# The last sequence through every expert with gates, the one before it in a group of three, and the retention's values multiplied once

## The chip, the cores and the metric

The kernel runs on one core of a Trainium2 chip. Its time is the device time of one execution in microseconds (us). Three runs of the kernel before took 1190.32, 1191.34 and 1193.39 us; the median is 1191.34. The profile is of one further execution, traced by the hardware profiler. PE is the engine that multiplies matrices, DVE the vector engine, ACT the scalar engine with its function tables, POOL the general engine that also issues the indirect transfers, and SP the queue that issues most other transfers. PSUM is the memory that PE writes here, and from which DVE and ACT read.

## The reference, cut to what matters

Sixteen sequences of 256 rows and 128 features go through two layers. Each layer is a mixer and an expert part, with a shift, a scale and a gate per sequence around both (adaLN).

```python
# layer 0: retention with 8 heads of 16, then experts that choose their rows
S = g * S + k_t[..., :, None] * v_t[..., None, :]
y_t = jnp.einsum('bhde,bhd->bhe', S, q_t)
...
top_p, top_idx = jax.lax.top_k(probs_et, cap)            # each of 8 experts takes 64 of 256 rows
...
# layer 1: a selective scan (256 inner features, 16 states), then rows that choose two experts
h = dA * h + dt_t[..., None] * b_t[:, None, :] * u_t[..., None]
y = jnp.einsum('bdn,bn->bd', h, c_t)
...
h = rms_weight * (x * jax.lax.rsqrt(var + EPS))
logits = jnp.einsum('bsh,eh->bse', h, gate_w)
top_w, top_i = jax.lax.top_k(scores, TOP_K)              # 2 of 8
top_w = top_w / jnp.sum(top_w, axis=-1, keepdims=True)
cw = jnp.einsum('tke,tk->te', oh, top_w.reshape(-1, TOP_K))   # weight of every expert for every row
a = jnp.einsum('th,eih->eti', hf, w1)
g = jnp.einsum('th,eih->eti', hf, w3)
eo = jnp.einsum('eti,ehi->eth', jax.nn.silu(a) * g, w2)
out = jnp.einsum('eth,te->th', eo, cw)
```

In this last part the weight of an expert that a row did not choose is zero, so a kernel may compute the chosen two experts only, or all eight and multiply by the weight.

## The kernel before, in words

**How the order of the work is set.** The program is written as chains (`pl.chain`), each with a number from the table `U`. A chain is a list of instructions; `need` names an event that must have happened, `done` announces one, and `take` and `give` hand buffers around as tokens. `Plan.issue` (line 320) goes through all chains with a time for every instruction from the table `USUAL`, always issues what can start first, and among what can start within 0.15 us on that engine takes the chain with the lowest number. The outcome is one fixed order per engine. Where PE would be idle beyond an allowance, it puts matmuls of zeros (line 384) in; these stop after the last sum of the scans (`h.pad = False`, line 1514).

**Layer 0.** Sequences go in four groups of four. `scores(b)` (line 773) makes queries and keys with features on the partitions, and the values with rows on the partitions. A head has 16 features, and the kernel multiplies in blocks of 32 partitions, so two heads share a block: the keys are masked once for the even and once for the odd heads (`ke`, `ko`), and the values are needed twice as well, with the other head's columns at zero. Before, the value weights are laid out twice (`wveo`, made by POOL in line 717, 256 columns), so that the product `pv` comes out as [even heads, odd heads] with zeros; ACT copies all 512 elements to `v`. The state between the two chunks of 128 rows is `kd` times the even half plus `kd` times the odd half, two matmuls (lines 826 and 827). `outputs0` (line 862) takes blocks of 32 columns of `v`. The expert part follows (`choose`, `gather`, `hidden`, `outputs`, `scatter`).

**Layer 1, scan.** `front(b)` makes the scan's inputs, `scans` (line 1413) runs 256 steps of 128 by 512, sixteen to a sequence, in order of the sequences: ACT makes `dA`, POOL `dB`, DVE scans in place and multiplies by C, and PE sums (`ya`). `back(k)` (line 1525) handles the pair of sequences 2k and 2k+1: projection, norm and residual. Its statistics are DVE's; the reciprocal root (`inv_std`, line 543: two instructions and three Newton steps of four) and the additions to `X` are POOL's.

**Layer 1, experts.** `GROUPS` (line 32) collects the pairs: 0 to 5 by two, and 6 and 7 alone. `prepare(k)` (line 1565) makes the pair's normed rows, the squares' mean with a second reciprocal root, the rows `hs` to be sent and the logits. `route(g)` (line 1619) picks two experts per row and gives every row a place in a list sorted by expert, padded to tiles of 128 rows: with c chunks of 128 rows there are 2c + 7 tiles. `send(g)` (line 1698) scatters the rows to DRAM by 2c indirect transfers. `expert(g, j)` (line 1723) loads one tile, transposes it, multiplies by `w1` and `w3` of the tile's expert (PE reads its number into a register), forms the gated product (`sl`, two buffers; ACT's tanh, two DVE instructions), transposes it in four pieces (`pm`, copied to `mT`, two buffers), multiplies by `w2`, and stores 128 rows. Odd tiles of the last group use the PSUM banks that the scans have left. `combine(k)` (line 1803) gathers each row's two results by indirect transfers, weighs and adds them and stores the output. The groups have 8, 8, 8, 4 and 4 chunks, so 23, 23, 23, 15 and 15 tiles, 99 in all.

The three lines that set the groups and tiles are these:

```python
GROUPS = ((0, 1), (2, 3), (4, 5), (6,), (7,))
CGS = [len(ks) * T // P for ks in GROUPS]
NJS = [2 * c + E - 1 for c in CGS]
```

## Time and profile before

| what | value |
|---|---|
| median of 3 runs | 1191.34 us |
| profiled execution, its own time | 1200.99 us |
| its span, first to last instruction | 1199.0 us |
| PE busy | 1059.6 us (88%), of it matmuls of zeros in the scans 153.5 us |
| DVE busy | 888.1 us (74%) |
| ACT busy | 764.3 us (64%) |
| POOL busy | 784.2 us (65%) |
| first scan starts | 230.7 us |
| last scan and its product end | 1041.6 us |
| 64 scatters, 64 gathers (indirect, POOL) | 64.9 us, 62.1 us |
| last tile's product stored from | 1177.1 us |

Busy times of engines overlap. A busy PE is not PE at its peak, because matmuls are pipelined and their ends are modelled; the distance between two starts says more. The clock is the share of full speed that PE was granted. Idle time of an engine that nothing waits for costs nothing. In rows of instructions the columns are start, duration, engine, line, operation, what is written from what, shape and count; many rows carry line 237, the helper that records every operation, so they are told apart by the names of their tiles.

### The profile page before, as it was taken

The numbers are of one execution on the slowest core, as the hardware profiler recorded it, in microseconds if no ns is written. First come the engines' busy times: TensorE is split into PE (matmuls) and PEld (weight loads), VectorE is DVE, ScalarE is ACT, GpSimd is POOL, SyncE is SP. The second block draws the span as 40 slices with busy tenths as digits, with TensorE's granted clock in tenths as the row PEclk, the third lists the DMA queues.
The fourth block names the chain that finished last, engine by engine and source line by source line (L and its number), as shares of the span: only waits on it lengthen the run. The fifth ranks groups of instructions, "written<-read, shape, count | busy, mean of one in ns | idle before, by whom it ended". The sixth has DMA issues, their size and how long they took to land.

```text
span 1199.0 us, 23439 instructions
## 1 busy us (share of the span) xinstructions
PE 1059.6 (88%) x7589; PEld 757.8 (63%) x7589; DVE 888.1 (74%) x1835; ACT 764.3 (64%) x1717; POOL 784.2 (65%) x1307
## 2 busy tenths in 40 slices
PE   9999999989898898799797898899988999988882
PEld 7767687767475665566565566667655766565661
DVE  5688804888989679977877897889878899835331
ACT  4555546677686787647755776678765786564451
POOL 4532303668685789569786888786886888664355
PEclk9999999999998999899899999899999999999996
DMA  6108232784585946656549652446334555221222
GB/s 198 16 28 223 86 108 80 192 207 141 144 220 145 280 124 152 167 145 176 147 124 226 169 135 74 112 133 162 103 91 121 155 141 134 80 63 51 73 73 59
DMA packets 122355, 157.61 MB, mean 131 GB/s; under 512 B 18756, under 2 KB 92300, under 8 KB 121868
## 3 DMA queue, kind: packets, MB, share of 16 engines
q1 hardware_dynamic: 117004, 140.90, 44.3%
q0 software_dynamic: 4096, 8.40, 2.7%
q10 hardware_dynamic: 1136, 6.82, 1.8%
q8 instruction: 64, 1.05, 0.4%
q14 instruction: 55, 0.45, 0.1%
HBM read 128.11 MB, written 27.96 MB: 130 GB/s over the span
## 4 chain that ended last, share of the span: by engine, by line
PE 44%; DVE 23%; POOL 10%; issue 8%; ACT 8%; DMA 6%; another core or an unknown queue 0%; SPq 0%; POOLq 0%; DVEq 0%; ACTq 0%
DVE dB L237 10%; PE py L1787 5%; PE pa L1757 5%; PE ya L237 4%; PE pg L1757 4%; PE ya L384 3%; PE pxs L237 3%; DMA rep<-dd 3%; DMA pr<-spd 2%; PE pm L237 2%; PE ph L237 2%; POOL dB L237 2%; DVE sl L237 2%; PE pye L237 2%; PE py L237 2%
## 5 line engine op out<-in xcount | busy, mean ns | idle before, releaser
L237 POOL TENSOR_TENSOR dB<-rep,bt 128x512 f32<-128x512 f32 x256 | 327.9, 1303 | 98.2 <-PE ya L237 71.4
L237 DVE TENSOR_TENSOR_SCAN dB<-dA,dB 128x512 f32<-128x512 f32 x256 | 310.2, 1216 | 52.9 <-ACT dA L237 25.9
L237 ACT ACTIVATE dA<-rep,A 128x255 f32<-128x255 f32 x512 | 222.2, 470 | 91.6 <-DVE dB L237 86.4
L384 PE MATMUL ya<-nought 128*128 128x256 bf16 x1122 | 153.5, 284 | 20.9 <-DVE dB L237 20.9
L237 DVE TENSOR_TENSOR dB<-dB,ct 128x512 f32<-128x512 f32 x256 | 168.6, 670 | 1.3 <-PE ct L237 1.1
L384 PEld LDWEIGHTS <-nought 128*128 128x128 bf16 x1270 | 129.1, 103 | 54.9 <-DVE dB L237 23.1
L1787 PEld LDWEIGHTS py<-w,mT 112*128 112x128 f32 x792 | 98.9, 192 | 49.2 <-ACT mT L237 26.5
L1787 PE MATMUL py<-w,mT 112*128 x792 | 108.6, 281 | 21.5 <-ACT mT L237 12.8
L237 DVE SCALAR_TENSOR_TENSOR sl<-sl,pa 128x448 f32<-128x448 f32 x99 | 60.9, 615 | 65.4 <-ACT sl L237 48.1
L1757 PE MATMUL pa<-w,xT 128*128 x198 | 97.8, 576 | 7.7 <-issue 2.5
L237 POOL DMA_INDIRECT got<-ydr,pos x64 | 62.1, 970 | 54.1 <-issue 19.4
L1757 PE MATMUL pg<-w,xT 128*128 x198 | 91.6, 544 | 0.0
L237 ACT ACT_TABLE_LOAD x66 | 84.7, 1283 | 10.8 <-DVE dB L237 4.4
L1705 POOL DMA_INDIRECT disp<-hs,pos x64 | 64.9, 1014 | 37.9 <-DVE pos L237 15.5
L237 PE MATMUL ya<-dB,c 128*32 128x512 f32 x512 | 78.8, 635 | 9.9 <-DVE dB L237 7.8
L237 ACT COPY mT<-pm 112x512 f32<-112x512 f32 x99 | 57.7, 584 | 35.0 <-PE pm L237 24.4
L237 DVE TENSOR_TENSOR sl<-sl,pg 128x448 f32<-128x448 f32 x99 | 61.5, 621 | 9.5 <-PE px L237 0.2
L237 ACT ACTIVATE sl<-pa 128x448 f32<-128x448 f32 x99 | 53.2, 542 | 23.2 <-PE pa L1757 18.7
L237 ACT ACTIVATE yt<-py 128x128 f32<-128x128 f32 x99 | 27.2, 276 | 62.8 <-PE py L1787 44.6
L237 PE MATMUL ph<-xin,fw 128*128 128x256 f32 x256 | 65.4, 391 | 1.0 <-ACT xin L237 0.8
L237 PE MATMUL pye<-fw,hg 128*64 128x128 f32 x1024 | 63.1, 276 | 0.5 <-ACT hg L237 0.5
L237 PE MATMUL pm<-c,sl 128*112 128x128 f32 x396 | 61.7, 276 | 1.4 <-ACT yt L237 0.7
(322 smaller groups left out, 2151.2 us busy)
## 6 DMA issues: line engine op xcount, KB each, us to landing
rep<-dd SPq DMA_DIRECT2D x128, 512.0 KB
fw<-in_fw SPq DMA_DIRECT2D x64, 256.0 KB
gt<-spd SPq DMA_DIRECT2D x64, 128.0 KB
pr<-spd SPq DMA_DIRECT2D x64, 128.0 KB
dd<-dx SPq DMA_DIRECT2D x16, 512.0 KB
xt<-disp SPq DMA_DIRECT2D x99, 64.0 KB
ydr<-yt SPq DMA_DIRECT2D x99, 64.0 KB
w<-in_w ACTq DMA_DIRECT2D x3, 1792.0 KB
```

What stands on the lines that cost most here:

```text
L237: i = getattr(real, name)(*args, **kw)
L384: self.nc.tensor.matmul(pad[:, 0:256], self.nought, self.spare, start=False, stop=False, skip_group_check=True)
L1705: i = nc.gpsimd.indirect_dma_start(out=disp[g], out_offset=bass.IndirectOffsetOnAxis(ap=pos[g][:, c, r, :], axis=0), in_=hss[GROUPS[g][c / ...
L1757: nc.tensor.matmul(o, xT, w[:, bass.ds(which[0], 1), :].rearrange("p o i -> p (o i)"), start=True, stop=True)
L1787: nc.tensor.matmul(py, mT[:, ic, :], w2[:, bass.ds(which[0], 1), ic, :].rearrange("p o d -> p (o d)"), start=(ic == 0), stop=(ic == NFC - 1),)
```

## The change

Three things change, and with them the table `U`.

- The pairs become a list: seven pairs, then sequence 14 alone and sequence 15 alone (`PAIRS`; nine entries). The fourth group takes pair 6 and sequence 14, so 6 chunks and 19 tiles. Sequence 15 is in no group. `back`, `prepare` and `combine` work on one or two sequences.
- Sequence 15 goes through `every_expert`: no routing, no scatter, no gather. Both of its chunks go through all eight experts, 16 products, each weighed by the gate, which is zero for experts that a row did not choose, and all summed in one PSUM bank. The rows' reciprocal root is not applied to the rows ahead of `w1` and `w3` but put into the tanh's scale (`half`) and the gate. For this sequence the reciprocal roots and additions of `back` and `prepare` run on DVE in place of POOL. The 69 tiles of the first three groups stay; with 19 and 16 there are 104.
- The values are multiplied once: the product has 128 columns, and ACT puts even and odd heads into a buffer [even, zeros, odd] whose zeros are written once. Blocks [even, zeros] and [zeros, odd] are read as overlapping slices. The state is one matmul.
- All numbers of `U` are other ones. The small buffers of statistics over two chunks have one copy in place of two (`few`). Odd tiles of the last group take the transposition's bank from `ps_y` in place of `ps_c`, which now holds the dense sum.

The diff, cut to its core:

```diff
+PAIRS = tuple((2 * k, 2 * k + 1) for k in range(7)) + ((14,), (15,))
+NB = len(PAIRS)
-GROUPS = ((0, 1), (2, 3), (4, 5), (6,), (7,))
+GROUPS = ((0, 1), (2, 3), (4, 5), (6, 7))
...
-         rep=50.85, exp=32.88, dB=104.34, ct=434.95, sum=89.24, scan=422.0, hC=369.42, yg=-40.53,
+         rep=242.95, exp=221.94, dB=152.25, ct=623.44, sum=-12.0, scan=527.94, hC=397.52, yg=31.12,
...
-CGS = [len(ks) * T // P for ks in GROUPS]
+CGS = [sum(len(PAIRS[k]) for k in ks) * NCH for ks in GROUPS]
...
-    wveo = fixed1(at, [P, 2, D], "wveo")
+    vz = [fixed1(at, [P, NCH, 4, 3, DH], f"v{i}") for i in range(2)]
...
+            for v in vz:
+                G.memset(v[:, :, :, 1, :], 0.0)
...
                 T_.matmul(
-                    pv[:, ch, :], hT[:, ch * P : (ch + 1) * P], wveo.rearrange("p q d -> p (q d)"),
-                    start=True, stop=True, us=0.43,
+                    pv[:, ch].rearrange("p j q e -> p (j q e)"), hT[:, ch * P : (ch + 1) * P], wv,
+                    start=True, stop=True, us=0.25,
                 )
-            v = vs[b] = at.tile([P, NCH, 2 * D], F32, tag="v", name=f"v{b}")
-            S.copy(v, pv)
+            v = vs[b] = vz[b % 2]
+            S.copy(
+                v[:, :, :, 0:3:2, :].rearrange("p c j q e -> p (c j) q e"), pv.rearrange("p c j q e -> p (c j) q e"), us=0.42
+            )
...
-            T_.matmul(pk[:, 1, :], kd, v[:, 0, 0:D], start=True, stop=False, us=0.25)
-            T_.matmul(pk[:, 1, :], kd, v[:, 0, D : 2 * D], start=False, stop=True, us=0.25)
+            T_.matmul(pk[:, 1, :], kd, v[:, 0, :, 0:3:2, :], start=True, stop=True, us=0.25)
...
-                            py[r, ch, :], vs[b][:, ch, par * D + 32 * j : par * D + 32 * j + 32], prs[b, j][:, ch, par, :],
+                            py[r, ch, :], vs[b][:, ch, j, par : par + 2, :].rearrange("p q e -> p (q e)"), prs[b, j][:, ch, par, :],
...
     def back(k):
+        W, kind = (V, "late") if k == NB - 1 else (G, None)
...
     def prepare(k):
+        dense = k == NB - 1
+        W, kind = (V, "late") if dense else (G, None)
...
+        if dense:
+            xTd = fa.tile([P, n * L], F32, tag="xTd", name="xTd", bufs=1)
+            S.activation(xTd, hT, AF.Copy, scale=rms)
+            done("xTd")
...
+    def every_expert(k, got):
+        xTd, lg, rr = got
+        b = PAIRS[k][0]
+        pl.chain(U['gated'])
+        need(("lg", k))
+        m8, i8 = fs.tile([P, NCH, 8], F32, tag="dm8", name="dm8"), fs.tile([P, NCH, 8], U32, tag="di8", name="di8")
+        for c in range(NCH):
+            V.max(m8[:, c, :], lg[:, c, :])
+            V.max_index(i8[:, c, :], m8[:, c, :], lg[:, c, :], us=0.3)
+        half, d2, ws, w0 = (fs.tile([P, NCH], F32, tag=t, name=t) for t in ("dhalf", "dd2", "dws", "dw0"))
+        V.tensor_scalar(half, rr, 0.5, None, ALU.mult)
+        done("half")
...
+        for r, (o, w) in enumerate(((gate, w0), (part, d2))):
+            V.tensor_tensor(o, iF[:, :, r].unsqueeze(2).to_broadcast([P, NCH, E]), io, ALU.is_equal)
+            V.tensor_tensor(o, o, w.unsqueeze(2).to_broadcast([P, NCH, E]), ALU.mult)
+        V.tensor_tensor(gate, gate, part, ALU.add)
+        for f in (rr, half):
+            V.tensor_tensor(gate, gate, f.unsqueeze(2).to_broadcast([P, NCH, E]), ALU.mult)
+        done("gate")
+        acc = ps_c.tile([P, NCH, D], F32, tag="c", name="accd")
+        for e in range(E):
+            for c in range(NCH):
+                n = NCH * e + c
+                pl.chain(U['dense'] + n / 100)
+                need("xTd", "half", "weights", ("yg", B - 1))
...
+                if n:
+                    need(("begun_", n - 1))
+                x = xTd[:, c * P : (c + 1) * P]
+                T_.matmul(pa, x, w1[:, e, :], start=True, stop=True)
+                done(("begun_", n))
+                T_.matmul(pg, x, w3[:, e, :], start=True, stop=True)
+                sl = fa.tile([P, FI], F32, tag="sl", name=f"sl_{n}")
+                S.activation(sl, pa, AF.Tanh, scale=half[:, c : c + 1])
+                V.scalar_tensor_tensor(sl, sl, 1.0, pa, ALU.add, ALU.mult)
+                give(ta)
+                need("gate")
+                V.scalar_tensor_tensor(sl, sl, gate[:, c, e : e + 1], pg, ALU.mult, ALU.mult)
...
+                for ic in range(NFC):
+                    T_.transpose(pm[:, ic, :], sl[:, ic * FC : (ic + 1) * FC], ident, us=0.16)
...
+                S.copy(mT, pm)
...
+                for ic in range(NFC):
+                    T_.matmul(
+                        acc[:, c, :], mT[:, ic, :], w2[:, e, ic, :], start=(n == 0 and ic == 0),
+                        stop=(e == E - 1 and ic == NFC - 1), skip_group_check=True,
+                    )
+                done(("dense", n))
+        pl.chain(U['dense'] + 1)
+        need(("dense", NCH * E - 1), ("x2", k))
...
+        V.tensor_tensor(res, acc, both(tab[:, 0, :]), ALU.mult, kind="fres")
+        V.tensor_tensor(res, res, X[b], ALU.add, kind="late")
+        Q.dma_start(rows_of((b,)), res)
...
-        for k in range(NHS, NB):
+        for k in range(NHS, NB - 1):
             prepare(k)
+        every_expert(NB - 1, prepare(NB - 1))
```

The numbers of `U` that the prediction speaks of order the tail: `tile` is (164.88, 54.77, 166.68, 110.24, -86.25) before and (328.09, 371.73, 101.71, -70.25) after, `dense` is -39.78 and `gated` -57.2.

## The prediction

> **What bounds the kernel now.** I read the sums by stage first, with stretches cut at the first scan (230.7 us), at the scan steps of sequences 13, 14 and 15, at the last scan's end (1040.4), at the first expert tile of the last group (1122) and at the last tile's end (1177). Columns: stretch, its length, busy us of PE, weight loads, DVE, ACT, POOL, then granted clock, DMA share, GB/s.
>
> ```profile
> core 0: us, PE busy (x) PEld busy (x) DVE busy (x) ACT busy (x) POOL busy (x), PEclk, DMA share, GB/s
> 0.00:230.70 230.70, 221.93 (x2173) 171.14 (x2174) 142.12 (x487) 124.33 (x266) 80.33 (x282) 1.00 0.40 112
> 230.70:867.70 637.00, 559.80 (x3871) 400.20 (x3870) 534.86 (x909) 452.21 (x976) 487.41 (x722) 0.96 0.60 158
> 867.70:937.90 70.20, 61.52 (x331) 39.91 (x330) 55.98 (x121) 43.62 (x108) 52.22 (x60) 0.98 0.42 112
> 937.90:989.20 51.30, 48.72 (x290) 33.10 (x289) 45.07 (x73) 40.39 (x100) 44.78 (x68) 1.00 0.56 145
> 989.20:1040.40 51.20, 47.68 (x273) 31.03 (x272) 48.78 (x101) 32.57 (x85) 40.17 (x52) 1.00 0.41 109
> 1040.40:1122.00 81.60, 71.21 (x395) 48.33 (x393) 37.25 (x106) 40.81 (x107) 40.48 (x84) 1.00 0.22 59
> 1122.00:1177.00 55.00, 48.77 (x267) 34.10 (x265) 22.24 (x41) 28.52 (x74) 25.39 (x29) 1.00 0.29 78
> 1177.00:1199.00 22.00, 0.00 (x0) 0.00 (x0) 1.76 (x5) 1.83 (x6) 13.48 (x16) 0.54 0.21 57
> ```
>
> Three regimes. Up to the first scan PE is full (222 of 231 us, DVE 62%). The scans, 810 us for 16 sequences, 50.6 each, are shared by PE, DVE and POOL; in the last step DVE has 48.8 of 51.2 us. After the last scan come 159 us in which DVE is under half busy and PE works on expert tiles, and 22 us at the very end in which PE does nothing at all.
>
> PE's instructions in the retention's steady loop show why its first stage is full: nothing stands between them but 0.18 us.
>
> ```profile
> 29.65 0.61 PE L237 MATMUL pk<-v,kd 128*128 128x128 f32 x4
> 30.10 0.60 PE L237 MATMUL pqk<-hTa,pk 128*128 128x256 f32 x2
> 30.53 1.03 PE L237 MATMUL pv<-wveo,hTa 128*128 128x256 f32 x4
> 31.39 0.38 PE L237 MATMUL pta<-c,xna 128*128 128x128 f32 x2
> 31.95 0.64 PE L237 MATMUL py<-pr,v 128*32 128x128 f32 x16 [0.18 <-ACT ko L237]
> ```
>
> From start to start the value projection takes 30.53 to 31.39, 0.86 us, and the state product 29.65 to 30.10, 0.45 us.
>
> The tile rows give the tail's load: 35 tiles after 1040.4, of them 16 after 1122.
>
> ```profile
> L237 ACT COPY mT<-pm x35: 562/586/590, 1045.2 to 1174.9; 112x512 f32<-112x512 f32 x35
> L237 ACT COPY mT<-pm x16: 573/586/590, 1126.4 to 1174.9; 112x512 f32<-112x512 f32 x16
> ```
>
> The chain of the tail, cut to what ended late, shows one tile's PE pieces and what the last group waits for.
>
> ```profile
> 1087.16 0.81 PE pl L237 x8
> ...
> 1121.80 0.30 PE px L237
> ...
> 1126.03 0.75 PE pg L1757 x2
> 1126.78 0.44 PE pm L237 x4
> 1127.32 0.76 PE pa L1757 x2
> 1128.08 0.75 PE pg L1757 x2
> 1128.83 0.89 PE py L1787 x8
> ```
>
> The gate's matmuls of sequences 14 and 15 (pl) end at 1088; the first tile's transpose starts 34 us later. Between lie the routing (8 us of small DVE instructions), eight scatters and the way through DRAM. Then 16 tiles run at 48.5/15 = 3.23 us each, while their PE pieces sum to 0.76 + 0.75 + 0.44 + 0.89 + 0.11 = 2.95. Behind the last one stand the gathers:
>
> ```profile
> 1177.07 1.53 DMA ydr<-yt
> ...
> 1191.19 2.50 DMA got<-ydr,pos
> ```
>
> **The change, part by part.** The sum is made against the profiled execution, span 1199.0 inside 1200.99 us; the median of the runs shown is 1191.34, 9.65 less, so I carry the difference over to the median.
>
> 1. Retention. The value projection has half the columns (0.86 to 0.43 us per sequence), the state product one matmul in place of two (0.45 to 0.22): 0.65 x 16 = 10.4 us of PE. All of it stands before the first scan. Where PE is the chain it is a gain. By the chain, PE holds most of 0 to 75 (8 sequences) and 145 to 231 (2 sequences), and a quarter of 75 to 145 (6), which DVE's top-8 rounds and POOL's chain set: 8 x 0.65 x 0.85 + 2 x 0.65 x 0.8 + 6 x 0.65 x 0.25 = 6.4. I take -6; ends 0 (all of it becomes filler matmuls) and -10.4. ACT's copy of the values has 256 elements, in runs of 16, for 512: between the q copy's 0.37 and its own 0.59, hidden beside PE either way. The POOL copies of the weights (2 x 0.23 us at 6 us) go; two memsets of the zero columns come, under the first loads.
>
> 2. Scan stage. The last steps take over back, prepare and route of sequence 14, which in before lay after 1040 with sequence 15. On DVE that is 4 statistics, 4 aggregates, one product of 0.42 and six chunks of routing, some 3 us more, in a step where DVE has 2.4 us free; eight scatters (1.27 us apart) leave the same step. I take +2. The priorities of all chains (table U) are new, and they reorder work on engines that are 80 to 95% full; nothing in the trace prices that. Bounds: the shortest steps are 40 to 44 us, the long ones 68.6 and 70.2 (sequences 10 and 13, with expert tiles and DVE waits inside), so one step's swing, -20 to +20.
>
> 3. First dense tile. In before the step from the last scan's end to the logits' end is 1088.2 - 1040.4 = 47.8. With one sequence instead of two: pom 1.3 less, its copy 0.2, normalising 0.8, two sets of statistics 1.1, norm and transposition in prepare 1.4, squares 0.8, second sequence's product and addition 2: -7.6. The three reciprocal roots move from POOL (16 instructions 0.28 apart, 1052.4 to 1057.0) to DVE, whose small ones stand 0.20 to 0.22 apart: -1.1 each, -3.3. X's updates: six POOL instructions (4.2 us) become three of about 0.42 on DVE, -3. Then two max/index pairs (0.34 each) and the halved scale: +1. 47.8 - 13.9 + 1 = 35 us. These DVE chains stand in line with two 0.62 us products per running tile, which the 0.3 to 0.6 us gaps of a DVE under half busy take. What runs meanwhile: the tiles left of the third group. In before sequence 13's scan ended at 937.9 and its tiles began 105 us later, so the first of the 35 tiles, less group six's 15 and group seven's 15, are 5 to 7 left over, 7 x 3.23 = 23 us, inside the 35.
>
> 4. The group of three. Its rows start when sequence 14's scan ends, 51 us before the last one. From scan end to first tile before took 105 us (12 and 13, in the scans) and 81.6 (14 and 15, in the tail). Half of this way lies in each now, with twelve scatters for eight (+5) but one sequence to prepare (-7): about 90, or 39 us after the last scan's end; close to the dense tiles' 35. Bounds 28 to 56. The extra scatters on POOL hold back only the gathers of the group before, which nobody waits for yet.
>
> 5. Tiles from there. 19 of the group and 16 dense. A routed tile costs 3.23. A dense one has no transpose of its rows (0.11), no load, no copy to xT, no result copy and no store: 2.84 of PE pieces against 2.95, and the same two products on DVE. I take 3.1 as the mean of both: 35 x 3.1 = 108.5. Bounds: 2.9 (PE back to back, -7) and 3.9, the whole tail of before with its waits (136.6 us over 35 tiles; +28); nearer the first, since from here on no tile waits for routing. The SP queue carries 88 loads and 88 stores of rows for 99, and one more of each table and of the output; none of it stands ahead of a tile for longer than now.
>
> 6. The end. In before 22 us follow the last tile: store, gathers 1.27 apart, sums, store. A dense end has the copy and py (1.8), two DVE instructions (0.9) and the store, which took 3.2 from issue to the span's end: about 5 after the last dense PE piece, if the twelve gathers and the sums of the group lie under the dense tiles.
>
> Tail: 35 + 108.5 + 5 = 148.5 against 158.6, -10. Sum: -6 + 2 - 10 = -14, or 1177 us. The removed 22 and the removed waits (81.6 to 35) are worth more than 60 us; most goes back because only 7 tiles, not 20, can run in the shadow, and the 104 tiles are five more than 99.
>
> One rule speaks against the change: the Trainium skill, page "TensorE: Matmul & The Clock Gate", Part 1, says that an idle window of about 3.4 us halves PE's clock until a busy one has passed. The filler matmuls stop with the last sum, and 35 - 23 - 4 leaves PE some 8 us idle before the first dense tile. The trace has the clock at 1.00 through 1040 to 1177, with no gap that long. By the rule the first tiles would lose about 1.7 us, an estimate from that page, and the sum would be -12.
>
> **The rivals.** *The gain is larger.* The tile pace goes to PE's 2.9 (-7), the first tile comes at 30 (-5) and the scans lose 6: 1159. For it: the two kinds of tiles wait for different things; against it: both take from the same two product and two transposed buffers, which set 3.23 today.
>
> *The group of three ends last.* If its tiles run among the dense ones to the end, the store and the gathers stand bare: 22 us less 5, up to +17. For: its rows come as late as the dense ones. Against: its priority stands before the dense tiles'. Half of it is +9: 1186.
>
> *Slower: a scan step is stretched.* Place: the steps of sequences 14 and 15, which now hold the preparation of the group of three on DVE (95% busy) and POOL. If one goes from 51 to the 70 of sequence 13, +19: 1196. It decides from +14 on. For: both 70 us steps are such mixtures. Against: steps 14 and 15 hold the same kind of work now and took 51.
>
> **How the numbers follow.** Main case 0.46 (own range 1165 to 1189), larger gain 0.22, group last 0.14, stretched step 0.18. A measurement here tells 0.3%, 3.6 us, from no change. Faster: 0.45 + 0.22 + 0.09 = 0.76; same 0.01 + 0.04 + 0.02 = 0.07; slower 0.01 + 0.16 = 0.17. For 8 in 10 the range reaches through the larger gain and to just past the stretched step's 1196: 1152 to 1198.
>
> **What would show it.** Right: pv and pk rows of half the sum, a first scan at 224 to 226; first dense tanh 30 to 40 us after the last scan; no gather after the last py; 5 to 6 us between that and the end. Wrong: a first scan at 230; gathers in the last 10 us; the scans' 810 us changed by over 10, which would outweigh the tail and make the forecast wrong in either direction.

## The result and the profile after

The changed kernel takes 1192.67 us (median of 17 executions, 1191.02 to 1198.13), the kernel before 1189.02 us (17 executions beside them): ratio 1.0039, 95% interval 1.0023 to 1.0054. It is slower by 0.3 to 0.4 per cent, where I had forecast 1177 us and a gain. A later measurement of both gave 1191.75 against 1189.31, ratio 1.0028 (1.0002 to 1.0054).

The first profile of the kernel before (span 1199.0) was of an execution of 1200.99 us, 12 us over this median. A second profile of it has the span 1185.4 inside 1187.26 us; of the 13.6 us between the two, 10.5 lie in the scans (799.2 in place of 809.7 us) and 2.6 in the tail (156.0 in place of 158.6), which is the stretch from the last scan to the end. I compare with this second one.

The sums by stage of the kernel before, second profile, cut at the first scan, the last scan's end, and after the last tile. Columns as in the prediction: stretch, length, busy us of PE, weight loads, DVE, ACT, POOL, then granted clock, DMA share, GB/s.

```profile
0.00:230.20 230.20, 221.51 (x2173) 171.14 (x2174) 142.25 (x487) 124.18 (x266) 79.91 (x282) 1.00 0.39 112
230.20:1029.40 799.20, 713.17 (x4759) 503.23 (x4758) 683.92 (x1199) 568.26 (x1266) 624.34 (x899) 0.97 0.57 152
1029.40:1161.90 132.50, 118.96 (x652) 82.39 (x650) 59.43 (x146) 69.19 (x179) 65.54 (x112) 0.99 0.25 68
1161.90:1185.40 23.50, 1.16 (x8) 0.97 (x8) 2.11 (x6) 2.39 (x8) 13.46 (x16) 0.56 0.21 56
```

The same of the changed kernel, cut also at 1137, where its last routed tile ends and only dense tiles follow:

```profile
0.00:229.20 229.20, 219.34 (x2212) 169.23 (x2213) 140.57 (x484) 120.52 (x266) 78.66 (x280) 1.00 0.39 112
229.20:1019.70 790.50, 693.11 (x4694) 494.85 (x4691) 679.92 (x1152) 555.42 (x1241) 613.96 (x929) 0.97 0.55 150
1019.70:1137.00 117.30, 109.52 (x617) 76.91 (x617) 69.37 (x212) 62.75 (x160) 58.26 (x65) 1.00 0.28 76
1137.00:1185.50 48.50, 45.09 (x224) 26.08 (x222) 20.58 (x35) 18.19 (x36) 17.39 (x21) 1.00 0.13 36
1185.50:1190.80 5.30, 1.16 (x8) 0.97 (x8) 0.85 (x2) 0.21 (x1) 0.00 (x0) 0.77 0.08 25
```

The bare end shrank from 23.5 to 5.3 us, as the change intends. The first scan comes 1.0 us sooner, and from it to the last scan it is 8.7 us less. But from the last scan to the end it is 171.1 us in place of 156.0: 790.5 - 799.2 - 1.0 + 171.1 - 156.0 = +5.4, which is 1190.8 - 1185.4.

How this splits into scans and tail depends on the cut. A scan step is finished when DVE has multiplied it by C. DVE's last scan and the multiplications behind it, in the kernel before (second profile):

```profile
1028.17 1.22 DVE L237 TENSOR_TENSOR_SCAN dB<-dA,dB 128x512 f32<-128x512 f32 x1
1029.30 1.26 DVE L237 TENSOR_TENSOR dB<-dB,ct 128x512 f32<-128x512 f32 x2
```

and in the changed kernel:

```profile
1018.46 1.22 DVE L238 TENSOR_TENSOR_SCAN dB<-dA,dB 128x512 f32<-128x512 f32 x1
...
1032.68 0.68 DVE L238 TENSOR_TENSOR dB<-dB,ct 128x512 f32<-128x512 f32 x1
...
1034.53 0.68 DVE L238 TENSOR_TENSOR dB<-dB,ct 128x512 f32<-128x512 f32 x1
```

Here the last two multiplications stand 13 us behind the last scan: from 1020.1 to 1031.0 DVE does the routing of the group of three, with products of routed tiles in between. Cut at the last multiplication's end (1030.6 and 1035.2), the scans are 806.0 in place of 800.4 us, 5.6 longer, and what follows 155.6 in place of 154.8. So the 8.7 us are not a gain of the scans: that work stands behind the cut.

The tile rows show what stands in the tail. In the kernel before (second profile):

```profile
L237 ACT COPY mT<-pm x35: 560/585/587, 1033.9 to 1161.3; 112x512 f32<-112x512 f32 x35
```

In the changed kernel, and there from 1135 on:

```profile
L238 ACT COPY mT<-pm x48: 568/585/590, 1019.7 to 1185.1; 112x512 f32<-112x512 f32 x48
...
L238 ACT COPY mT<-pm x16: 585/585/586, 1134.9 to 1185.1; 112x512 f32<-112x512 f32 x16
```

48 tiles stand behind the last scan, not 35: five more are there in all (104 for 99), and eight that used to run ahead of it. Behind the last multiplication it is 44 tiles and 35. All 16 dense tiles come last, one behind the other, and PE is busy for 93% of both stretches.

In that dense stretch the chain that ended last goes round in a ring. One turn of it (start, duration, what):

```profile
1143.51 0.66 PE pm L238 x4
1144.25 0.58 ACT mT L238
1144.84 0.55 ACT sl L238
1145.41 0.63 DVE sl L238
1146.09 0.04 issue
1146.13 0.69 DVE sl L238
1146.82 0.04 issue
1146.87 0.66 PE pm L238 x4
```

A tile's transposition (pm) is copied by ACT (mT), ACT then does the next tile's tanh (sl), DVE its two products, and only then PE can transpose again: 3.36 us from pm to pm. My pace was 3.1.

### The profile page after: what moved, and what is told of

The parts are those of the page before. It is cut to its first block, busy times and chain, and to the rows that moved or that the text cites. A ratio compares the mean times of both kernels' runs of the same rounds, so it can differ in the third digit from the quotient of the medians.

```text
span 1190.8 us, 23613 instructions
## 1 busy us (share of the span) xinstructions
PE 1068.2 (90%) x7747; PEld 768.0 (64%) x7747; DVE 911.3 (77%) x1884; ACT 757.1 (64%) x1702; POOL 768.3 (65%) x1292
## 5 line engine op out<-in xcount | busy, mean ns | idle before, releaser
L385 PEld LDWEIGHTS <-nought 128*128 128x128 bf16 x1395 | 138.7, 101 | 44.7 <-DVE dB L238 14.8
L1806 PEld LDWEIGHTS py<-w,mT 112*128 112x128 f32 x704 | 87.3, 191 | 36.9 <-ACT mT L238 15.5
L1806 PE MATMUL py<-w,mT 112*128 x704 | 96.1, 281 | 12.0 <-ACT mT L238 4.7
L238 DVE SCALAR_TENSOR_TENSOR sl<-sl,pa 128x448 f32<-128x448 f32 x104 | 63.7, 613 | 43.3 <-ACT sl L238 42.7
L1776 PE MATMUL pa<-w,xT 128*128 x176 | 84.5, 562 | 4.7 <-issue 2.7
L238 PE MATMUL ya<-dB,c 128*32 128x512 f32 x512 | 75.0, 659 | 12.6 <-DVE dB L238 12.3
L238 POOL DMA_INDIRECT got<-ydr,pos x60 | 57.8, 963 | 37.8 <-DVE acc L238 15.6
L1776 PE MATMUL pg<-w,xT 128*128 x176 | 81.2, 543 | 0.0
L238 PEld LDWEIGHTS pm<-c,sl 128*112 128x112 f32 x416 | 47.2, 134 | 36.5 <-DVE sl L238 21.4
L238 PEld LDWEIGHTS pye<-fw,hg 128*64 128x64 f32 x1024 | 58.4, 140 | 14.8 <-DVE fres L238 5.8
L238 ACT ACTIVATE sl<-pa 128x448 f32<-128x448 f32 x88 | 46.8, 538 | 22.5 <-PE pa L1776 21.8
```

What stands on the lines that cost most here:

```text
L238: i = getattr(real, name)(*args, **kw)
L385: self.nc.tensor.matmul(pad[:, 0:256], self.nought, self.spare, start=False, stop=False, skip_group_check=True)
L1776: nc.tensor.matmul(o, xT, w[:, bass.ds(which[0], 1), :].rearrange("p o i -> p (o i)"), start=True, stop=True)
L1806: nc.tensor.matmul(py, mT[:, ic, :], w2[:, bass.ds(which[0], 1), ic, :].rearrange("p o d -> p (o d)"), start=(ic == 0), stop=(ic == NFC - 1),)
```

## The experiments

Where the text below says that an order is held, every instruction stands in the place that it has in the kernel named, with the same fillers; the filler matmuls are those of zeros. "Replanned" means that the planner makes a new order.

### Is the profile of before typical?

*before_again*: the kernel before once more, unchanged.

> The kernel before, profiled once more, because its first profile (span 1199.0 us) lies some 12 us above the span that its median of 1189.02 stands for. If the excess was in the tail, the last scan ends near 1040 here as well and the tail is near 147 us; if it was in the scans, the last scan ends near 1028 and the tail stays at 155 to 160. I expect the second: span 1187 +- 4, first scan 230 to 231, scans 798 +- 6, tail 157 +- 3.

It took 1187.26 us, with the scans 799.2 and the tail 156.0 as expected. So the tail of 158.6 us that I reckoned with was 2.6 us too long: against 156.0, my 148.5 us are a gain of 7.5 and not of 10, and the whole forecast is -11.5 and not -14.

### What is the shorter retention worth?

*values_once_held*: the retention part alone on the kernel before, order held.

```diff
-    pv[:, ch, :], hT[:, ch * P : (ch + 1) * P], wveo.rearrange("p q d -> p (q d)"),
+    pv[:, ch].rearrange("p j q e -> p (j q e)"), hT[:, ch * P : (ch + 1) * P], wv,
...
-T_.matmul(pk[:, 1, :], kd, v[:, 0, 0:D], start=True, stop=False)
-T_.matmul(pk[:, 1, :], kd, v[:, 0, D : 2 * D], start=False, stop=True)
+T_.matmul(pk[:, 1, :], kd, v[:, 0, :, 0:3:2, :], start=True, stop=True)
```

> The retention's part alone, with every engine's order and all filler matmuls as in the kernel before. The prediction's reading (PE is the path of the first stage): first scan 6 us earlier, 224 to 226, and 5 to 6 us off the time, ratio 0.995. The rival (PE waits elsewhere, the freed time becomes idle time on PE): first scan at 229 to 230, time within 2 us of before.

1188.43 us, ratio 1.0001 (0.9977 to 1.0025). The instructions are as short as they should be. These are PE's groups ahead of 260 us, shape by shape (busy us, mean ns, idle before), in the kernel before:

```profile
L237 PE MATMUL pv<-wveo,hTa 128*128 128x256 f32 x64 | 17.2, 384 | 0.0
L237 PE MATMUL pk<-v,kd 128*128 128x128 f32 x64 | 11.0, 290 | 0.5 <-ACT hg L237 0.4 <-DVE kd L237 0.2
```

and with the retention part:

```profile
L237 PE MATMUL pv<-pk,hTa 128*128 128x128 f32 x64 | 10.5, 279 | 0.0
L237 PE MATMUL pk<-v,kd 128*128 128x128 f32 x32 | 7.0, 301 | 0.5 <-ACT hg L237 0.4 <-DVE kd L237 0.2
```

10.7 us less by these rows, and ACT's copy of the values went from 593 to 380 ns. The stage's row shows what came of it:

```profile
0.00:228.70 228.70, 216.04 (x2141) 166.38 (x2142) 142.06 (x486) 120.77 (x266) 79.64 (x282) 0.99 0.40 112
```

PE is busy for 5.5 us less, and the first scan starts at 228.7, only 1.5 us sooner: 4 us of it are new idle time of PE, so the end of that stage is set by more than PE's work. The other 5 us of the saving went into fillers and matmuls that took longer. The granted clock stood at 0.50 from 47 to 50 us, where the kernel before has 1.00 in the whole stage. The 1.5 us themselves are no more than what one and the same first stage varies by (229.2 to 231.3 us, see the last section). The scans (801.0) and tail (157.6) are those of before within 2 us. The rival had it, not my theory.

*values_once_planned*: the same part, replanned with the table `U` of the kernel before; the planner is told the shorter durations.

```diff
-    start=True, stop=True, us=0.43,
+    start=True, stop=True, us=0.25, kind="pvn",
```

> The retention's part alone, and the order is worked out anew with the shorter durations. If the planner turns the freed time into an earlier end: ratio 0.994 to 0.997. If it fills it: about 30 to 40 filler matmuls more ahead of the first scan, first scan at 228 to 231, ratio 0.997 to 1.004; what differs then comes from the new order of the scans, in either direction.

1257.97 us, ratio 1.061 (1.0579 to 1.0642): first scan 242.4, last scan's end 1066.1, tail 189.2. The instructions are those of the run before, save that the planner put 207 fillers ahead of the first scan in place of 149 (by the traces), so the 69 us between the two are the order and its fillers.

*values_refitted*: the same part, replanned with a table searched for it (two of its numbers as an example).

```diff
-U = dict(... scan=422.0, hC=369.42 ...)
+U = dict(... scan=2251.24, hC=398.8 ...)
```

> The retention part alone on the kernel before, with the table of urgencies searched anew for it: from the table of before, numbers moved at random and kept where the planner counted no later an end. Theory (the 69 us that the same part cost with the old table came from a plan that nobody had fitted, and the shorter retention itself is worth nothing): the loss goes, and nothing comes in its place: 1186 to 1194, ratio 0.997 to 1.005, first scan 227 to 231. Rival A (the retention's 6 to 10 us are real, and only the held order hid them): 1178 to 1183, first scan at 224 or earlier. Rival B (the retention's new form itself is bad for the later stages, with its two zeroed buffers used in turn and the strided ACT copy): over 1200 still.

1213.93 us, ratio 1.0207 (1.0181 to 1.0233): 44 of the 69 us came back, and 25 did not. The first scan is at 230.9 and the tail 159.1, so the loss is in the scans, 821.9 us. My theory expected none. Rival B falls too, because in the held order the same new form left scans and tail alone. What is shown is that this table is worse than the one before; whether another would close the gap is open.

*gates_once_held*: the reverse, the old retention put back on the changed kernel, order held. The diff is that of values_once_held with the signs turned, and POOL's copies stand elsewhere:

```diff
+    if not ch:
+        add_to_last(halves, ahead=True)
```

Here `halves` are POOL's two copies into `wveo`, issued ahead of the first value product.

> The changed kernel with the retention of the kernel before put back (each value matrix multiplied twice, two product matmuls for the state, the plain ACT copy) and every engine's order kept as in the changed kernel, so that the rest of the change stands alone: the last sequence dense, the group of three, and the plan made for them. Theory (the shorter retention is worth nothing, because what PE gains before the first scan it spends waiting or on fillers; the slower time is all from the tail): within 2 us of the changed kernel, 1191 to 1195, ratio to the kernel before 1.002 to 1.005; first scan still at 229 +- 1.5 us; fewer fillers than the changed kernel's 35 us of them before the first scan. Rival (the retention does bring the 6 us that I forecast, and the tail costs 10): about 1198, ratio 1.008 or more, with the first scan at 233 or later.

1201.85 us, ratio 1.0114 (1.0067 to 1.016), first scan at 240.6: the rival's numbers. But the trace has something else in it. PE's row of the first value product, and the row after it:

```profile
14.46 1.23 PE L238 MATMUL pv<-wveo,hTa 128*128 128x256 f32 x4 [1.98 <-POOL wveo L738]
15.48 1.06 PE L385 MATMUL pad<-nought 128*128 128x256 bf16 x4
```

and stretches of this run (the last three figures are clock, DMA share, GB/s):

```profile
12.00:16.00 4.00, 2.02 (x10) 1.25 (x9) 2.47 (x13) 1.39 (x4) 2.32 (x10) 0.92 0.83 231
16.00:20.00 4.00, 4.00 (x31) 2.92 (x30) 0.57 (x5) 1.85 (x5) 0.64 (x4) 0.50 0.55 158
20.00:24.00 4.00, 3.99 (x20) 2.87 (x20) 2.77 (x5) 1.02 (x2) 1.57 (x8) 0.50 0.20 31
24.00:28.00 4.00, 4.00 (x42) 2.70 (x41) 0.00 (x0) 1.93 (x5) 1.46 (x6) 0.80 0.10 1
```

My edit had left POOL's two copies of the value weights just ahead of the first product. PE waited 2 us for them, and the granted clock stood at 0.50 for some 8 us afterwards. The first output of the retention (the copy yT) came at 27.8 in place of 20.3 us: 7.5 of the 11.4 us were made there. The run did not measure what it was made for.

*gates_held_fewer*: the same with up to 80 fillers fewer (156 in place of 231 by the trace); `debt` grows by five with each sequence.

```diff
-                for _ in range(warm):
+                less = min(warm, self.debt)
+                self.debt -= less
+                for _ in range(warm - less):
```

> The old retention on the changed kernel, orders held, as in the run before, but after each sequence's second state matmul the next five filler matmuls are left out (80 in all, as many as the changed kernel has more than the kernel before ahead of the first scan). Theory (the freed PE time only became fillers: with the old retention and fewer fillers PE's order is as full as it was before, and the first scan comes when the other engines let it): first scan at 229 to 232, time 1190 to 1195, ratio 1.001 to 1.005. Rival (the shorter retention is worth 9 us in this order, whatever the fillers): first scan at 238 to 241, 1199 or more.

Median 1197.46 us, ratio 1.0051 (1.0023 to 1.0079), first scan at 236.5, neither theory's number, with the same 2 us wait in it.

*gates_clean* and *gates_clean_fewer*: both again, with POOL's copies where the kernel before has them.

```diff
-    if not ch:
-        add_to_last(halves, ahead=True)
...
+                if key == "G" and "it_a" in (h.out or ""):
+                    self.seen += 1
+                    if self.seen == 4:
+                        self.extra()
```

(`extra` is `halves`.)

> The old retention on the changed kernel, orders held and fillers kept, with POOL's two copies of the value weights after its sixth operation of the first normalisation, where the kernel before had them (ready at 6.6 us there), in place of just ahead of the first value product (ready at 14.4 us in the earlier run). Theory (of the 11.4 us by which the first scan was late, 7.5 came in the first 28 us, from that wait and the clock at .50 behind it; the longer products themselves cost the other 3.9): clock 1.00 ahead of 28 us, first scan at 232 to 234, time 1193 to 1198. Rival (the longer products cost it all, and the clock would have fallen anyway): first scan at 238 to 241, time 1199 or more.

> The same with 80 filler matmuls fewer ahead of the first scan, five after each sequence's second state product. Theory (the longer products then take the fillers' place): first scan at 229 to 232, 0 to 2 us behind the changed kernel's; time 1191 to 1195. Rival (the products are in the way whatever stands in the gaps): the same first scan as with the fillers kept, 232 to 234, or later.

The clock now stands at 1.00, and the first scan comes at 234.7 with the fillers kept and at 234.1 with fewer. The stretches with the fillers kept:

```profile
16.00:20.00 4.00, 3.67 (x33) 2.66 (x36) 2.78 (x5) 2.03 (x6) 2.57 (x13) 1.00 0.82 241
20.00:24.00 4.00, 4.00 (x75) 3.19 (x68) 1.81 (x5) 1.78 (x5) 0.96 (x5) 1.00 0.13 5
```

So the longer products cost 5.3 us of the changed order's first stage and the wait with the clock behind it cost the other 6 (as far as the first stages of two chips can be compared), and it matters little whether fillers stand between them. Whole times can't be read here: both runs (1217.61 and 1217.03, ratios 1.0168 and 1.0172) were made on another chip, where the kernel before took 1198.78, and have a tail of 186 and 187 us, with two pauses of PE, 2.6 and 6.6 us long, that the other runs of this order don't have in that place.

*after_again*: the changed kernel unchanged, to see what it varies by.

> The changed kernel once more, as it is. Theory (its first stage does not vary, and the longer tail of the last two runs belongs to their measurement and not to the retention): first scan at 228.5 to 230; the ratio to the kernel before 1.002 to 1.006 if the tail is 171 us again, and up to 1.013 if it is the 186 us of the last two runs, where the old retention's share is then 4 to 6 us. Rival (the longer tail came from the old retention): tail 171 and ratio 1.002 to 1.006 even with the kernel before at 1195 or more beside it.

1191.75 us against 1189.31, first scan 229.4, scans 790.3, tail 171.0: within 0.2 us of its first profile in every stage. It was measured beside a kernel before of 1189, not of 1199, so by itself it says nothing on the longer tail of the last pair. Two earlier runs do: *gates_once_held* and *gates_held_fewer* have the old retention too, and tails of 171.2 and 171.3 us. So the old retention does not make the tail longer; what did on that chip stays open.

### Do the fillers hold the first scan back?

*fillers_half* and *fillers_none*: the changed kernel without every second filler, and without any, ahead of the first scan. The edit is that of the second; the first has `warm // 2` in place of 0.

```diff
-                for _ in range(warm):
+                for _ in range(0 if at["T"] < 229 else warm):
```

> The changed kernel with every second filler matmul ahead of the first scan left out (about 143 of them), all else in its order. Theory (PE's fillers stand in gaps that other engines leave, and the first scan at 229 is set by these): first scan 228 to 230, time 1190 to 1194. Rival A (the fillers take longer than the gaps they are meant for, 145 ns each in the trace in place of the 111 ns counted in the kernel's own text, and hold back the work behind them): first scan 224 to 226, time 1186 to 1189. Rival B (with fewer fillers the granted clock falls and PE's work gets longer): a clock under 1.00 in the windows ahead of the first scan, first scan at 231 or later.

> The changed kernel without any filler matmul ahead of the first scan (those behind it stay). Theory (gaps only, but the clock needs some work in them): a granted clock under 1.00 in some window ahead of the first scan, where PE's real work then takes longer; first scan 229 to 236. Rival A (fillers hold back real work, and the clock does not need them here, since PE's real work alone is .84 of the time): clock 1.00 throughout, first scan 222 to 226, time 1184 to 1189. Rival B (nothing changes: neither the clock nor the first scan): 228 to 230.

Median 1196.13 us, ratio 1.0068 (1.0042 to 1.0095), and 1194.89 us, ratio 1.0071 (1.0042 to 1.01). The first scan comes at 236.1 and 236.3, seven later. Without any filler PE has longer gaps, and its trace shows this:

```profile
51.73 1.23 PE L238 MATMUL po<-pk,yn 128*128 128x128 f32 x4 [5.30 <-ACT yn L238]
52.89 1.08 PE L238 MATMUL py<-pr,v 128*32 128x128 f32 x16
```

and its stretches this:

```profile
28.00:100.00 72.00, 60.01 (x651) 45.78 (x647) 47.79 (x176) 32.94 (x79) 25.82 (x100) 0.83 0.26 64
100.00:236.30 136.30, 127.74 (x1131) 96.48 (x1130) 77.86 (x246) 75.62 (x158) 40.82 (x119) 0.99 0.40 118
```

Sixteen py matmuls take 1.08 us here, 0.64 at full clock. So the fillers pay in the first stage; rival B of the first run and the theory of the second have it. In the profiles, though, the seven us are gone at the last scan, which ends at 1019.4 and 1016.8 (1019.7 in the changed kernel): the scans took 783.3 and 780.5. I have not found out why. The medians are 3.5 and 2.2 us above the changed kernel's, and the intervals of the ratios overlap with its own (1.0023 to 1.0054), so that the fillers pay in the whole is likely and not shown.

### What holds the tail?

*tanh_first*: in the dense tiles ACT does the next tile's tanh ahead of this tile's copy.

```diff
                 S.activation(sl, pa, AF.Tanh, scale=half[:, c : c + 1])
+                done(("tanh_", n))
...
+                if n < NCH * E - 1:
+                    need(("tanh_", n + 1))
                 mT = fa.tile([FC, NFC, P], F32, tag="mT", name=f"mT_{n}")
```

> The changed kernel, only that ACT does tile n+1's tanh ahead of tile n's copy in the dense tiles. New theory (the 13 dense tiles alone at the end go round a ring of transposes 0.66, copy 0.58, tanh 0.55, products 0.63 and 0.69, 3.35 to 3.65 us in all, because the copy stands ahead of the next tanh on ACT): the pace falls to PE's 2.9 to 3.0 and the time to 1185 to 1187, 6 us under the changed kernel's 1192.67 and ratio 0.997 to before. Rival (PE sets the pace, its work is what it is): no change, 1192 to 1194, ratio 1.003 to 1.004.

1191.06 us, ratio 1.0024 (1.0003 to 1.0044). The pace of the dense tiles is 46.9 / 15 = 3.13 us, so the ring is what the chain said; but the whole gains 1.6 us, where the theory gave about six, and even that lies within the two intervals. PE's own pieces are probably next: in the changed kernel's chain, pa and pg stand at 0.75 each, pm at 0.45 and the product with `w2` at 1.14, 3.1 in all, and with the early tanh PE is busy for 44.6 of the 47.0 us from 1143.5 on.

*dense_half*: the changed kernel without the dense products of experts 4 to 7, order held (with `mute` an instruction keeps its place in the plan and is not issued).

```diff
                 pl.chain(U['dense'] + n / 100)
+                pl.mute = e > 3
```

> The changed kernel without the dense tiles of experts 4 to 7 (8 of 16 tiles left out, so sequence 15 lacks these experts' share); every other instruction keeps its place. Theory (the whole way from the last scan to the end goes tile after tile, 3.4 us each): 8 x 3.42 = 27 us less, 1163 to 1168. Rival (the sums of the group of three, whose last store is issued at 1181.9 of 1190.8, end it anyway): 3 to 8 us less, 1184 to 1190.

1178.59 us, ratio 0.9921 (0.9885 to 0.9956). The last dense copy comes at 1158.7, 26.4 us sooner for eight tiles, 3.3 each. Only 14 us arrive at the end. The rows there:

```profile
1169.15 0.38 SPq L239 DMA_DIRECT2D out<-acc  x1
1169.62 0.42 SPq L239 DMA_DIRECT2D fres<-rowd  x1
1172.84 0.42 DVE L239 TENSOR_TENSOR resd<-accd,fres 128x256 f32<-128x256 f32 x1 [5.38 <-DMA fres<-rowd]
```

The last dense product ends at 1161.4. The sums of the group of three are a second chain, whose last store is issued at 1169.15, 8 us later, and the residual rows for the last sequence are loaded behind that store: DVE waits 5.4 us for them.

*routed_less*: the changed kernel without the work of the last five of the 19 routed tiles, order held; other rows stand where their results would.

```diff
         pl.chain(U['tile'][g] + j / 100)
+        less = g == NG - 1 and j >= NJS[g] - 5
...
+        pl.mute = less
```

> The changed kernel without the work of the last five of the 19 tiles of the group of three (their loads stay, other rows are stored in the place of their results); the order is held. Theory: the five tiles by which 104 exceeds 99 cost a full pace each, 5 x 3.4 = 17 us, 1174 to 1178. Rival (there is slack around the routed tiles, only the dense ring at the end counts): under 5 us, 1188 to 1192.

1188.7 us, ratio 0.9997 (0.9977 to 1.0017): 4 us less for five tiles. Counted from the last scan (1025.6 in this profile), the last routed tile's result came 16.4 us sooner, but the first dense copy only 7.0. Between them ACT's rows are these:

```profile
1127.33 0.40 ACT L239 ACTIVATE acc<-got,wts 128x128 f32<-128x128 f32 x1 [4.31 <-DMA out<-acc]
1130.23 0.40 ACT L239 ACTIVATE acc<-got,wts 128x128 f32<-128x128 f32 x1 [2.50 <-DMA got<-ydr,pos]
```

and PE's

```profile
1132.65 1.10 PE L239 MATMUL pm<-c,sl 128*112 128x128 f32 x4 [7.22 <-DVE sl L239]
```

In the fixed order ACT's weighted sums stand ahead of the dense tiles' tanh, and wait for gathers and for a store. Most of the time taken out of the routed tiles is given back there.

*no_last_gather*: the kernel before without the gathers and the weighted sums of its last pair, order held.

```diff
         pl.chain(U['comb'][g])
+        pl.mute = k == NB - 1
```

> The kernel before without the gathers and the sums of its last pair of sequences (the experts' share of sequences 14 and 15 is left out, their rows are doubled and stored); the order is held. It prices the bare end. Theory: 22 us fall to 4 to 6, so 16 to 18 us less than before, 1171 to 1174. Rival (the store behind it or the sums of the pair before stand there as well): 5 to 10 us less.

1173.79 us, ratio 0.9877 (0.983 to 0.9924): the bare end was worth 15 us, near what I had counted.

### Is it the plan?

*old_urgencies*: the changed kernel replanned with the table of the kernel before, and its last expert group's number for the dense tiles.

```diff
-U = dict(gated=-57.2, dense=-39.78, load0=4.7, ...)
+U = dict(gated=-25.65, dense=-86.25, load0=-80.57, ...)
```

> The changed kernel with the table U of the kernel before (the two new entries: gated as its last prepare, dense as its last tile). Theory (the table fits one plan; any other plan loses tens of us, as the retention alone did with 1258): 1215 to 1265. Rival (the structure sets the time, the table only breaks ties): 1185 to 1200.

1268.46 us, ratio 1.0665 (1.0607 to 1.0724), with scans of 812.4 and a tail of 225.4 us. A table fits one set of instructions: both replanned runs with an unfitted one lost 69 to 76 us against the same instructions in a fitted order.

*after_refitted*: the changed kernel with a table searched from there.

```diff
-U = dict(gated=-57.2, dense=-39.78, ...)
+U = dict(gated=185.49, dense=2365.42, ...)
```

> The changed kernel with another table of urgencies, searched from the table of before (which gave 1268 us): same instructions, another order. Theory (five more tiles, 104 in place of 99, and a bound work on the engines in the scans and behind them: the plan decides only where the tiles run, and the sum of scan stage and tail stays): 1187 to 1196, with the tiles split differently between the scans and the tail, the scan stage 3 to 5 us longer or shorter for every four tiles that it takes in or loses, and the tail the other way. Rival (the changed kernel's time is a matter of its table alone, and the structure would bring the 12 us that I forecast in another plan): 1180 or less, ratio 0.993 or less.

1192.64 us, ratio 1.0033 (1.0009 to 1.0057): another order, the same time as the changed kernel's to 0.1 us, with 46 tiles in the tail (171.4 us) and scans of 789.4 us.

*refitted_tanh_first*: the same search with the early tanh; its diff is that of tanh_first and another table.

> The same search on the changed kernel with one more edit: in the dense tiles ACT does the tanh of tile n+1 ahead of the copy of tile n. With the changed kernel's own table that edit was worth 1.6 us (ratio 1.0024 in place of 1.0039) and brought the dense pace from 3.42 to 3.17 us. Theory (the dense tiles' ring is a small part; routed tiles, sums and PE's own work hold the tail as well): 1 to 3 us under the run with the same search and without the edit, 1186 to 1194; dense pace 3.1 to 3.2 us. Rival (with a plan made for it, the ring is what held the tail): 1180 or less, tail under 160 us.

1191.55 us, ratio 1.0018 (0.9996 to 1.0039). Its stages:

```profile
0.00:229.20 229.20, 220.40 (x2192) 170.78 (x2193) 141.59 (x486) 120.95 (x266) 79.24 (x281) 0.99 0.38 109
229.20:1027.50 798.30, 708.89 (x4719) 496.98 (x4717) 679.84 (x1185) 569.08 (x1265) 613.96 (x928) 0.96 0.55 150
1027.50:1191.50 164.00, 140.99 (x770) 98.11 (x768) 84.26 (x213) 73.00 (x173) 75.75 (x85) 0.97 0.22 61
```

Five more tiles in the scans (61 for the changed kernel's 56), the scans 7.8 us longer, the tail (43 tiles) 7.1 us shorter: the sum of the two stays within 1 us. Here too the split is one of the cut: at the last multiplication's end the two stages are 807.0 and 155.3 us, 1.0 and 0.3 us from the changed kernel's. Four orders of these instructions (the changed kernel's, tanh_first and these two) end within 1.6 us of one another, and none beats the kernel before. That supports the theory that the amount of work, and not one bad order, keeps the changed kernel at 1191 to 1193. Four orders are not all orders.

## Why the prediction was wrong, step by step

Three terms failed: the retention (-6, and 1.0 measured), the pace of the tiles (108.5 us, and 114.9 measured), and the way to the first tile, which came out at 50.5 us for 35 and by another mechanism than I had described.

**Retention, -6 (ends 0 and -10.4).** PE's saving was right: 10.7 us by the rows. The first scan came 1.0 us sooner, at 229.2, close to the 230 that I had named as the sign of "wrong". In the order of before the saving was worth 1.5 us; the other engines' chains set the pace more than the shares I gave them (0.85 and 0.8 of the saving, where PE held the chain) allowed. In the changed order, the longer products would cost 5.3 us (measured on another chip). So this order needs the shorter products just to keep the first scan where it was; what it spends the 4 us on was not tried.

**Scan stage, +2 (bounds -20 to +20).** Measured -8.7 to the last scan and +5.6 to its last multiplication, both inside the bounds. I treated the scans as a stage of their own, but tiles and routing move across its end: eight tiles left it, the last two multiplications slid behind 11 us of routing, and both came back behind the last scan. With the old table the same changes cost 76 us more: 22 in the scans, still inside the bounds, and 54 in the tail.

**First dense tile, 35, and the group's first tile, 39.** This step failed in its mechanism. I let dense and routed tiles run mixed and took the tiles left of the third group for 5 to 7, "in the shadow". There were 13 (nine behind the last multiplication). The fourteenth copy, the group's first, came at 1070.2, 50.5 us after the last scan, and PE was busy for 47.1 of the first 50.3 us. There was no shadow left to fill. The first dense tanh came at 1131.6, 112 us after the last scan and behind all 19 routed tiles; I had written 30 to 40. Even the weights that a dense tile needs (dgate) were ready only at 1114.5. They were no limit, though: in after_refitted they are ready at 1071.0, the first dense tanh still comes at 1132.2, and the time is the same. As a number the step did less harm, because it holds the work that had left the scans: there the time is 10.7 us under my +2, here 15.5 over my 35, which leaves 4.8 us, and only 0.8 against the 39 that I had for the group's first tile. That the two nearly cancel is luck.

I had also said that the extra scatters would hold back only gathers that nobody waits for. POOL's rows show it the other way round:

```profile
1049.44 0.97 POOL L238 DMA_INDIRECT got<-ydr,pos  x1 [0.30 <-issue]
1050.72 0.99 POOL L1723 DMA_INDIRECT disp<-hs,pos  x1 [0.31 <-issue]
1052.01 0.97 POOL L238 DMA_INDIRECT got<-ydr,pos  x1 [0.30 <-issue]
1053.28 0.99 POOL L1723 DMA_INDIRECT disp<-hs,pos  x1 [0.30 <-issue]
```

Scatters alternate with gathers of an earlier group: 12 of them took from 1031.3 to 1060.7, 29 us in place of the 15 that twelve steps of 1.27 make. Since 13 tiles were waiting, PE did not run dry over it.

**Pace, 3.1 for 35 tiles.** This term was mis-sized most. From the group's first copy to the last dense one it was (1185.1 - 1070.2) / 34 = 3.38: 3.38 for the routed tiles, 3.35 for the dense. The dense tile's shorter PE work (my 2.84) did not set its pace; the ring did, and without the ring it was 3.13. My PE sums were too small as well: they have 0.89 us for the product with `w2`, while the chain of before has 0.89 and 1.16 by turns.

**The end, 5.** From the last copy to the end 5.7. That step was right: the gathers ended at 1171.5 and no gather stood after the last tile. Taking away the bare end was worth 15 us by itself.

Tail: 50.5 + 114.9 + 5.7 = 171.1 against my 35 + 108.5 + 5 = 148.5. Of the 22.6 us between them 15.5 are the first term, 6.4 the second, 0.7 the third. Against the second profile of before my sum was -6 + 2 - 7.5 = -11.5, and +5.4 was measured. Of these 16.9 us, 5.0 are the retention, -10.7 + 15.5 = 4.8 the scans with the way to the group's first tile, 6.4 the pace and 0.7 the end. No one of them alone turns the sign; it takes the pace, the retention and part of the third.

**The clock rule that I weighed.** The Trainium skill, page "TensorE: Matmul & The Clock Gate", Part 1, let me estimate 1.7 us for a gap ahead of the first dense tile. There was no such gap: the clock in both tail stretches is 1.00.

**Rivals.** None of the three happened as written. "The group of three ends last" came nearest: its last sums are stored from 1181.9, 6 us ahead of the last sequence's, and a kernel with half the dense tiles ended on them. "A scan step is stretched" is right in its place and not in its weight: from the start of sequence 14's scan to the last multiplication it is 115.6 us in place of 103.6, 12 more, with the routing of the group of three inside. But the scans ahead of it are 6.4 us shorter, and this delay was not tried by itself. The 70 us of sequence 13's step that the rival reckons with are 63.7 in the second profile. The slower outcome got a chance of 0.17, nearly all on such a step, and none on the retention and the pace, where most of it arose.

## What to carry to other kernels

Work that disappears from a bare end has to be compared with the work that replaces it at that stage's own price: here PE's idle time behind the last scan went from 35.9 to 15.3 us (stretch less busy time), but its work there from 120.1 to 155.8, by five more tiles and eight moved ones. And a stage's time means little before it is known what was moved across the cut: the scans here are 8.7 us shorter by one cut and 5.6 us longer by the other. Before counting a freed engine's time as a gain, look for what else paces the stage: the same 10.7 us of PE were worth 1.5 us or nothing in one order and about 5 in another. And when an order is written out by a planner, compare changes with the order held and again with a fitted one; an unfitted order costs several times what is being measured, and a control must not move a wait to a new place.

## What the runs showed of the hardware

In *gates_once_held*, a wait of PE of 1.98 us was followed by a granted clock of 0.50 for 8 us and 0.80 in the four after them; the stretch that holds the wait has 0.92. In *fillers_none*, a wait of 5.3 us had 0.50 as well, from 48 to 56 us. But the length of one wait does not decide it in these runs: in *gates_held_fewer* PE waited 2.13 us at 54.4, and the clock stayed at 1.00, and in *values_once_held* it was 0.50 from 47 to 50 us, though PE's longest wait in the ten us before is 0.82. What does decide it was not tried. The page named above, Part 1, puts the idle window at about 3.4 us. By that rule the wait of 5.3 us can explain its drop, while one of 1.98 us is too short to fill a window. In the kernel before the clock stays at 1.00 in the whole stage.

A stage of the same program, ahead of the scans, can repeat within 0.5 us from one profile to another (229.2 and 229.4 for the changed kernel, 230.7 and 230.2 for the kernel before). But *tanh_first*, *routed_less* and *dense_half* have the changed kernel's instructions up to there, in its order, and their first scans come at 229.7, 230.2 and 231.3, so 2 us is the safer measure. The scans of one and the same program varied by ten (809.7 and 799.2 for the kernel before). A difference of less than that in one pair of profiles says nothing about the scans, and that holds for the -8.7 and the +5.6 of this change too.
